# Two layers on one core: where layer 1's output weights are folded, and when its first queries are made

## The chip, the cores and the metric

The kernel runs on one core of a Trainium2 chip. The metric is the device time of one execution in microseconds, lower is better. Before the change three executions took 1293.99, 1299.66 and 1301.15 us; the median is 1299.66.

## What is computed

Two transformer layers, all in float32, over 2 sequences of 1024 tokens with 256 features. Each layer adds an attention and a feed-forward network, both fed with the same normalized input. Layer 1's attention compresses keys and values to 64 numbers for each token (`kv`) and has 16 heads:

```
xn = layernorm(x)
q  = rmsnorm(xn @ wq_a.T) @ wq_b.T            # 16 heads: 128 plain + 64 rotated
kv = rmsnorm((xn @ wkv_a.T)[..., :64])        # shared by all heads
q_abs  = einsum(q_nope, q_absorb)             # 64 per head
scores = (q_abs . kv + rope(q_pe) . rope(k_pe)) * SCALE      # causal
attn   = softmax(scores)
x = einsum('bhst,btc->bhsc', attn, kv)
x = einsum('bhsc,hdc->bhsd', x, out_absorb)   # 64 -> 128 per head
attention = x.reshape(b, s, 16 * 128) @ wo.T  # -> 256
ffn = bitlinear(sigmoid(bitlinear(xn, w1)) * bitlinear(xn, w2), w3)
```

The last two lines of the attention are both linear, with nothing between them. So `out_absorb` and `wo` can be multiplied into one matrix of 64 x 256 for each head. That product of weights is one of the things that the change moves.

## The kernel before

The program is written in an order fixed by hand: inside `manual_schedule` each engine runs its instructions in the order in which the code issues them. It has two scopes, with their own pools in SBUF and PSUM. The first holds layer 0, layer 1's feed-forward network and the preparation of layer 1's attention. The second holds layer 1's attention. A tile of the second scope may lie where tiles of the first lay, and then it waits for their last readers.

**The end of the first scope.** A list `fill` holds the items of layer 1's feed-forward network, first the products with w1 and w2 (`up`, L686), then those with w3 (`down`, L703). After each item, one piece from a second list, `side`, is issued (`pump`, then `side.pop(0)()`). In `side` stand, in this order: normalization and keys, the queries' transposes of batch 0 (`queries1`), the eight calls of `fold`, and at the end the last transposes and the first two queries.

**`fold(p)`** treats a pair of heads. It multiplies the query weights by `q_absorb` (L832, into `wm` and `w2`) and `out_absorb` by `wo` (L840, into `wvo`), and copies the three results from PSUM with `copy_out` (L95 on VectorE, L99 on ScalarE, in turn). `fold_load` fetches the factors of a pair over SP's queue (L822), two pairs ahead. The `wo` factors lie where layer 0's context lay.

**A query** (`Query`) belongs to 128 tokens and 8 heads. `project` makes it on TensorE (L143, L150) into a pair of PSUM banks; ScalarE copies it out (L169, L157, L172); `rotate` multiplies it by cosine and sine and adds (L173, L174, L178). Its parameter `engines` has GpSimd as default, for all three. The first two queries are made in the first scope by `query(0)` and `query(1)`, and use two `temp` tiles each as room. GpSimd runs nothing else there.

**The second scope.** 16 steps, one for each (batch, pair of token blocks i and 7 - i, 8 heads). A step has four cycles `c`; each cycle treats two heads for both blocks:

- `scores` (L1180): TensorE into a PSUM pair (tag `s`, two of them, also used by `project` and the outputs), then VectorE adds the mask and takes the maximum (L1187), then ScalarE's exp (L1191);
- `turn_over` (L1197): VectorE transposes the weights into `pT`, of which there are two, one for each of two successive steps;
- `values` (L1228): the product of the previous step's `pT` with `vrep`, into the PSUM tile `o` (four banks). The first step has no previous step, so it has no such product;
- `output` (L1255): the step before the previous one, multiplied by `wvo`.

`vrep` is filled with 32 copies of 64 KB on SP's queue (L1131) at the border of the scopes. It takes the place of `x_sb`, so it starts after the last store of x (L710).

Of the kernel before, what the change touches and what calls it, by code (L numbers as in the profile page):

```python
# [46 lines left out]
def two_layers(ctx: ExitStack, tc: tile.TileContext, a: dict, out: bass.AP):  # L47
# [42 lines left out]
    def copy_out(dst, src, scale=None):  # L90

        turn[0] += 1
        if turn[0] % 2:
            if scale is None:
                nc.vector.tensor_copy(dst, src)  # L95
            else:
                nc.vector.tensor_scalar(dst, src, scale, None, ALU.mult)
        else:
            nc.scalar.activation(dst, src, AF.Copy, scale=1.0 if scale is None else scale)  # L99
# [94 lines left out]
    with ExitStack() as scope:  # L194
# [10 lines left out]
        def ps_bank():  # L205
            return ps0.tile([P, SC], F32, tag="m", name="ps_m", bufs=3)
# [599 lines left out]
        def fold_load(p):  # L806
            if p == 0:


                wm = main.tile([P, 2, NPAIR, P], F32, tag="wA", name="wm")  # L810
                folded["wm"], folded["w2"] = wm[:, 0], wm[:, 1]
                nc.sync.dma_start(folded["w2"][:R2], a["wpe2"])
                folded["wvo"] = main.tile([P, NPAIR, E], F32, tag="wB", name="wvo")
                folded["wo"] = l0.tile([P, 4, 2, E], F32, tag="ctx_n", name="fold_wo")
            t0 = l0t.tile([P, S], F32, tag="head0", name="fold0", bufs=3)
            t, at = {}, 0
            for key, width in (("wbn", LQ), ("wka", LKV), ("wva", LKV)):
                t[key] = t0[:, at : at + 2 * width].rearrange("p (h r) -> p h r", h=2)
                at += 2 * width
            t["wo"] = folded["wo"][:, p % 4]  # L820
            for key in ("wbn", "wka", "wva", "wo"):
                nc.sync.dma_start(t[key], a[key][:, 2 * p : 2 * p + 2, :])  # L822
            folded[p] = t

        def fold(p):
            if p + 2 < NPAIR:
                fold_load(p + 2)
            t = folded[p]
            pm = ps_bank()
            for lo, n, at in ((0, P, 0), (P, R2, P)):  # L830
                for hh in range(2):
                    nc.tensor.matmul(  # L832
                        pm[P - n :, at + hh * LKV : at + (hh + 1) * LKV],
                        t["wbn"][:, hh, lo : lo + n], t["wka"][:, hh, :], start=True, stop=True,
                    )
            copy_out(folded["wm"][:, p, :], pm[:, :P])
            copy_out(folded["w2"][R2:, p, :], pm[R2:, P : 2 * P])
            pv = ps_bank()
            for hh in range(2):
                nc.tensor.matmul(  # L840
                    pv[hh * LKV : (hh + 1) * LKV, :E], t["wva"][:, hh, :], t["wo"][:, hh, :],
                    start=True, stop=True,
                )
            copy_out(folded["wvo"][:, p, :], pv[:, :E])


        with tc.manual_schedule():

# [243 lines left out]
            while fill:  # L1092
                k = len(fill)
                pump()
                for _ in range(-(-len(side) // k)):
                    side.pop(0)()
                if k == 17:
                    wpe = main.tile([P, 8 * E], F32, tag="wC", name="wpe")

                    maskw = wpe[:, NPAIR * P + 4 * P :]  # L1100
                    trig = wpe[:, NPAIR * P : NPAIR * P + 4 * P].rearrange("p (k t) -> p k t", k=4)
                    wpe = wpe[:, : NPAIR * P].rearrange("p (r c) -> p r c", r=NPAIR)
                    nc.sync.dma_start(wpe, a["wpe"])
                    for k_, i in enumerate((TB - 1, 0)):
                        for x_, key in enumerate(("cosq", "sinq")):
                            nc.sync.dma_start(
                                trig[:, 2 * k_ + x_], a[key][:, i * P : (i + 1) * P]
                            )

                    maskw = maskw.bitcast(BF16)  # L1110
                    nc.gpsimd.memset(maskw[:, : S - P], 0.0)
                    nc.gpsimd.tensor_copy(maskw[:, S - P :], maskz[:, SC - P :])

                    def query(k):
                        q = ready[steps[0]][k]
                        q.project(ps_pair())
                        q.rotate(
                            room=[temp("t").rearrange("p (r t) -> p r t", r=QP) for _ in range(2)]
                        )

                    ahead(0)
                    last = [lambda c=c, n=n: queries1(1, c, n) for n in (0, 4) for c in range(2)]
                    side += last[:2] + [lambda: query(0), last[2], lambda: query(1), last[3]]
            while side:
                side.pop(0)()

# [20 lines left out]
    with ExitStack() as scope:  # L1147
# [9 lines left out]

        class Step:
            pass

        def new_step(b, i, g):
            s = Step()
# [108 lines left out]
        with tc.manual_schedule():  # L1271
            prev, older = None, None

            def values(n0, n1):
                for sb in range(n0, n1):
                    product(prev, sb)

            for at in range(len(steps)):
                s = new_step(*steps[at])
                nxt = ahead(at + 1) if at + 1 < len(steps) else ()  # L1280
                for c in range(NCY):
                    wide = [2 * c, 2 * c + 1]
                    share = (c * NSB // NCY, (c + 1) * NSB // NCY) if prev is not None else (0, 0)
                    if c == 0 and older is not None:
                        normalize(older, 0)
                        fetch_x(older)
                    scores(s, 0, wide[:1])
                    if c == 0:
                        if older is not None:
                            normalize(older, 1)  # L1290
                        if prev is not None:
                            inverse(prev)
                        scores(s, 0, wide[1:])
                        scores(s, 1, wide)
                        values(*share)
                    else:
                        values(*share)
                        scores(s, 1, wide)
                        turn_over(s, 0, wide[0])
                        scores(s, 0, wide[1:])  # L1300
                    k = c // 2
                    q, after = None, []
                    if c % 2 == 0:
                        if nxt:
                            q = nxt[k]
                            q.project(pair("t"))
                    elif prev is not None:
                        t = pair("t")
                        if older is not None:
                            after.append(output(older, k, t[:, 0, :E]))  # L1310
                        after.append(inverse_T(prev, k, t[:, 1]))
                    if c == 0:
                        turn_over(s, 0, wide[0])
                        turn_over(s, 0, wide[1])
                        turn_over(s, 1, wide[0])
                        turn_over(s, 1, wide[1])
                    else:
                        turn_over(s, 1, wide[0])
                        turn_over(s, 1, wide[1])
                        for f in after:  # L1320
                            f()
                        turn_over(s, 0, wide[1])
                    if q is not None:
                        q.rotate()
                older, prev = prev, s

            for k in range(2):
                normalize(older, k)
                if k == 0:
                    fetch_x(older)  # L1330
            inverse(prev)
            mid = prev.nsb // 2
            values(0, mid)
            for k in range(2):
                t = pair("t")
                after = [output(older, k, t[:, 0, :E]), inverse_T(prev, k, t[:, 1])]
                for f in after:
                    f()
                if k == 0:
                    values(mid, prev.nsb)  # L1340
            normalize(prev, 0)
            mid = (prev.nsb + NSB) // 2
            values(prev.nsb, mid)
            t = pair("t")
            output(prev, 0, t[:, 0, :E])()
            values(mid, NSB)
            normalize(prev, 1)
            t = pair("t")
            output(prev, 1, t[:, 0, :E])()
# [67 lines left out]
```

## Time and profile before

| | us |
|---|---|
| median of three executions | 1299.66 |
| the profiled execution | 1296.76 |
| its span, first to last instruction | 1293.8 |
| TensorE busy | 1254.8 |
| VectorE busy | 743.9 |
| ScalarE busy | 640.9 |
| GpSimd busy | 486.6 |
| granted TensorE clock, mean | 0.996 |

The profile comes from one execution. The rows of the timeline read: start in us, duration in us, engine, line of the program, operation, what is written and read, shapes, count; in brackets the idle time of that engine ahead of the row and what ended it. A float32 matmul appears as two records. Shapes such as 128*64 are the rows and columns of TensorE's array that it uses. PE is TensorE, DVE VectorE, ACT ScalarE, POOL GpSimd, SP the engine that issues most transfers. A row that merges several records ("x8") gives the time from the first one's start to the last one's end, and records of TensorE overlap.

### The profile page before, as it was taken

What the parts mean: (1) busy time and instruction counts of PE and PEld (TensorE: products, weight loads), DVE (VectorE), ACT (ScalarE), POOL (GpSimd) and SP (SyncE); (2) the same over time, 40 slices, a digit from 0 to 9 for tenths busy, and PEclk for the clock granted to TensorE, in tenths of its full rate; (3) what the DMA queues carried; (4) which work ended last, traced back from release to release, by engine and by line L of the source; (5) the groups of instructions that cost most, each with busy time, mean ns of one, the idle gap of its engine ahead of it and who ended that gap; (6) DMA issues with size and microseconds to landing.
All of it is one profiled execution on the core that took longest, in us unless ns stands there. A gap on an engine that the chain in (4) does not pass through costs nothing. (4 is left out here: it accounts for less than half of the span.)

```text
span 1293.8 us, 36603 instructions
## 1 busy us (share of the span) xinstructions
PE 1254.8 (97%) x15774; PEld 790.3 (61%) x15774; DVE 743.9 (57%) x1873; ACT 640.9 (50%) x1228; POOL 486.6 (38%) x512
## 2 busy tenths in 40 slices
PE   8999999999999999999998899999999999999997
PEld 6554644545546445365585567677666677777665
DVE  5956545655456564134335666676566666766663
ACT  4465456375465444433323555555555555555541
POOL 6662325253233221103315543354345434544320
PEclk9999999999999999999999999999999999999999
DMA  6421301001001000002124100000001000000000
GB/s 187 127 56 51 90 1 26 14 13 17 9 1 26 26 1 21 17 1 80 48 86 76 20 19 7 26 11 15 21 8 27 7 28 10 27 11 7 23 7 23
DMA packets 66113, 41.10 MB, mean 32 GB/s; under 512 B 37857, under 2 KB 63329, under 8 KB 65825
## 3 DMA queue, kind: packets, MB, share of 16 engines
q1 hardware_dynamic: 64960, 36.69, 11.2%
q8 instruction: 123, 2.02, 0.7%
q10 hardware_dynamic: 704, 1.05, 0.2%
q0 software_dynamic: 288, 1.05, 0.2%
q14 instruction: 38, 0.30, 0.1%
HBM read 26.18 MB, written 10.49 MB: 28 GB/s over the span
## 5 line engine op out<-in xcount | busy, mean ns | idle before, releaser
L1191 ACT ACTIVATE p<-p,nmax 128x1024 f32<-128x1024 f32 (+7 forms) x256 | 197.2, 771 | 205.3 <-DVE nmax L1187 204.5
L1180 PE MATMUL ps_s<-kT,qc 128*128 128x512 f32 (+3 forms) x768 | 278.6, 497 | 14.2 <-DVE nmax L1187 13.0
L1187 DVE CUSTOM_DVE_ANT_0 p<-ps_s,wpe 128x1024 f32<-128x1024 f32 (+7 forms) x256 | 184.8, 744 | 182.6 <-PE ps_s L1180 177.3
L461 ACT ACTIVATE p<-ps_s 128x1024 f32<-128x1024 f32 (+1 forms) x192 | 153.3, 808 | 166.7 <-PE ps_s L454 161.8
L1180 PEld LDWEIGHTS ps_s<-kT,qc 128*128 128x128 f32 x768 | 130.9, 190 | 123.2 <-issue 90.7
L1197 DVE STREAM_TRANSPOSE pT<-p 128x1024 f32<-128x1024 f32 (+7 forms) x256 | 186.5, 758 | 13.2 <-ACT p L1191 13.2
L413 PE MATMUL ps_m<-head,head 16*128 16x512 f32 (+3 forms) x672 | 177.8, 533 | 1.0 <-DVE nmx L424 0.6
L454 PE MATMUL ps_s<-head,head 17*128 17x512 f32 (+3 forms) x768 | 164.5, 533 | 0.0
L1228 PE MATMUL ps_o<-pT,vrep 32*64 32x128 f32 x9216 | 151.2, 275 | 4.8 <-DVE rinv L1202 2.6
L178 POOL TENSOR_TENSOR qc<-t,t 32x512 f32<-32x512 f32 x120 | 152.1, 1268 | 8.1
L1228 PEld LDWEIGHTS ps_o<-pT,vrep 32*64 32x64 f32 x9216 | 134.8, 131 | 32.2 <-issue 23.8
L464 POOL TENSOR_SCALAR_AFFINE_SELECT p<-p 128x256 f32<-128x256 f32 x128 | 53.5, 422 | 224.7 <-ACT p L461 223.5
L173 POOL TENSOR_TENSOR t<-t,cosq 128x512 f32<-128x512 f32 x28 | 35.6, 1272 | 259.7 <-issue 144.2
L413 PEld LDWEIGHTS ps_m<-head,head 16*128 16x128 f32 x672 | 67.7, 183 | 84.7 <-issue 27.8
L686 PE MATMUL ps_m<-xnT,w 128*128 128x512 f32 x192 | 92.3, 608 | 0.0
L429 DVE TENSOR_REDUCE nmx<-ps_m 128x1 f32<-128x512 f32 x112 | 72.2, 685 | 32.6 <-PE ps_s L454 24.6
L424 DVE CUSTOM_DVE_ANT_0 junk<-ps_m,maskz,nmx 128x512 f32<-128x512 f32 (+3 forms) x112 | 57.6, 548 | 47.1 <-PE ps_s L454 29.8
L479 PE MATMUL ps_o<-p,v 128*32 128x512 f32 (+3 forms) x768 | 81.6, 498 | 0.0
L567 PEld LDWEIGHTS ps_m<-wpr,hT 128*128 128x128 f32 x512 | 59.9, 191 | 17.9 <-DVE nmx L429 6.8
L424 DVE CUSTOM_DVE_ANT_0 junk<-ps_m,maskz 128x512 f32<-128x512 f32 (+3 forms) x112 | 50.5, 487 | 29.3 <-PE ps_s L454 24.6
L567 PE MATMUL ps_m<-wpr,hT 128*128 128x128 f32 x512 | 66.6, 282 | 0.0
L1255 PE MATMUL ps_t<-wvo,xT 128*128 128x256 f32 x256 | 62.6, 387 | 3.5 <-DVE nmax L1187 2.6
(179 smaller groups left out, 1739.4 us busy)
## 6 DMA issues: line engine op xcount, KB each, us to landing
stage<-rows SPq DMA_DIRECT2D x96, 64.0 KB, 3.1
rows<-proj SPq DMA_DIRECT2D x23, 256.0 KB, 2.4
w<-in_w SPq DMA_DIRECT2D x3, 768.0 KB, 5.1
x_sb<-in_x SPq DMA_DIRECT2D x4, 512.0 KB, 5.3
x<-x_sb SPq DMA_DIRECT2D x4, 512.0 KB, 3.2
fold_wo<-in_wo SPq DMA_DIRECT2D x8, 256.0 KB, 3.4
vrep<-kv SPq DMA_DIRECT2D x32, 64.0 KB, 2.1
xin<-x SPq DMA_DIRECT2D x16, 128.0 KB, 2.2
```

The source lines that it names most:

```text
L178: (even, odd)[x].tensor_tensor(self.qc[64 + 32 * x : 96 + 32 * x, hh], t1[at : at + 32], t2[at : at + 32], ALU.add,)
L413: nc.tensor.matmul(t[:, :w], quad(q, c, D0)[:, i * P : (i + 1) * P], quad(k, c, D0)[:, k0 : k0 + w], start=True, stop=True, tile_position= ...
L424: nc.vector.tensor_tensor_reduce(junk[:, :w], t[:, :w], maskz[:, SC - w :], -1.0, dst if k0 else 3.0e38, ALU.add, ALU.min, dst,)
L454: nc.tensor.matmul(t[:, c % 2, :w], quad(k, c, D0 + 1)[:, j * P : (j + 1) * P], quad(q, c, D0 + 1)[:, at : at + w], start=True, stop=True, ...
L461: nc.scalar.activation(p[:, pair[0] : pair[0] + 2, :w], t[:, :, :w], AF.Exp)
L567: nc.tensor.matmul(po[:, :P], f["h", hc // 2][:, hc % 2, t * P : (t + 1) * P], wpr[:, hc, cols], start=(hc == 0), stop=(hc == NH0 - 1),)
L686: nc.tensor.matmul(pw, w1t[f"w{i + 1}"][:, kc, hc * P : (hc + 1) * P], xnT1[n // 2][:, kc, (n % 2) * SC : (n % 2 + 1) * SC], start=(kc == ...
L1180: nc.tensor.matmul(sc[:, j * SC + n0 : j * SC + n1], s.q[k].qc[:, h // QP, h % QP, :], kT[:, s.b * S + n0 : s.b * S + n1], start=True, sto ...
L1187: nc.vector.tensor_tensor_reduce(p, sc[:, j * SC : j * SC + w], maskw[:, S - w :], -1.0, 3.0e38, ALU.add, ALU.min, nmax,)
L1191: nc.scalar.activation(p, p, AF.Exp, bias=nmax, scale=-1.0, accum_out=s.rsum[:, k, h : h + 1])
L1197: nc.vector.transpose(s.pT[:, at, h, :], s.p[k, h])
L1228: nc.tensor.matmul(s.o[64 * hh : 64 * hh + 64, c, k * P : (k + 1) * P], vrep[32 * c : 32 * c + 32, s.b * 32 + sb, :], s.pT[32 * c : 32 * c ...
```

## The change

Three edits.

1. `fold` no longer makes `wvo`, and `fold_load` no longer fetches its two factors (`wva`, `wo`).
2. A new function `output_weights` fetches both factors over GpSimd's queue, in five transfers of 512 KB, into a tile of the tag `pT`, which has two buffers, ahead of the first step. It returns eight pieces, one for each pair of heads, which multiply them into the PSUM tile `o`, and `take`, with which ScalarE copies the result to `wvo`. In the first step `fill` issues a piece at three places of cycles 1 and 3 and at two places of cycle 2; `take` follows the step.
3. Among the last pieces of `side`, `query(0)` and `query(1)` each change places with the transposes that stood ahead of them.

```diff
@@ fold_load
-                folded["wvo"] = main.tile([P, NPAIR, E], F32, tag="wB", name="wvo")
-                folded["wo"] = l0.tile([P, 4, 2, E], F32, tag="ctx_n", name="fold_wo")
...
-            for key, width in (("wbn", LQ), ("wka", LKV), ("wva", LKV)):
+            for key, width in (("wbn", LQ), ("wka", LKV)):
...
-            t["wo"] = folded["wo"][:, p % 4]
-            for key in ("wbn", "wka", "wva", "wo"):
+            for key in ("wbn", "wka"):
@@ fold
-            pv = ps_bank()
-            for hh in range(2):
-                nc.tensor.matmul(
-                    pv[hh * LKV : (hh + 1) * LKV, :E], t["wva"][:, hh, :], t["wo"][:, hh, :],
-                    start=True, stop=True,
-                )
-            copy_out(folded["wvo"][:, p, :], pv[:, :E])
@@ the last pieces of side
-                    side += last[:2] + [lambda: query(0), last[2], lambda: query(1), last[3]]
+                    side += [last[0], lambda: query(0), last[1], lambda: query(1)] + last[2:]
@@ second scope
+        def output_weights():
+
+            t = att.tile([P, NSB, NH2, 32], F32, tag="pT", name="wov", bufs=2)
+            t = t.rearrange("p n h q -> p (n h q)")
+            wo = t[:, : NH * E].rearrange("p (h e) -> p h e", h=NH)
+            wva = t[:, NH * E : NH * (E + LKV)].rearrange("p (h d) -> p h d", h=NH)
+            nc.gpsimd.dma_start(wva, a["wva"])
+            for h in range(0, NH, 4):
+                nc.gpsimd.dma_start(wo[:, h : h + 4], a["wo"][:, h : h + 4])
+            folded["wvo"] = main.tile([P, NPAIR, E], F32, tag="wB", name="wvo")
+            pv = ps.tile([P, 4, SC], F32, tag="o", name="ps_wvo").rearrange(
+                "p k (x e) -> p (k x) e", e=E
+            )
+
+            def product(p):
+                for hh in range(2):
+                    nc.tensor.matmul(
+                        pv[hh * LKV : (hh + 1) * LKV, p, :], wva[:, 2 * p + hh, :],
+                        wo[:, 2 * p + hh, :], start=True, stop=True,
+                    )
+
+            def take():
+                for k in range(0, NPAIR, 4):
+                    nc.scalar.copy(folded["wvo"][:, k : k + 4, :], pv[:, k : k + 4, :])
+
+            return [lambda p=p: product(p) for p in range(NPAIR)], take
@@ the steps
+            fold, fold_take = output_weights()
+
+            def fill():
+                if c > 0 and fold:
+                    fold.pop(0)()
...
                         values(*share)
+                        fill()
                         scores(s, 1, wide)
+                        fill()
                         turn_over(s, 0, wide[0])
                         scores(s, 0, wide[1:])
+                        if c != 2:
+                            fill()
...
+                if at == 0:
+                    fold_take()
```

## The prediction

> **What bounds the kernel now.** I read the page first: busy shares, then the 40 slices.
>
> ```profile
> PE 1254.8 (97%) x15774; PEld 790.3 (61%) x15774; DVE 743.9 (57%) x1873; ACT 640.9 (50%) x1228; POOL 486.6 (38%) x512
> ...
> PE   8999999999999999999998899999999999999997
> ```
>
> TensorE is busy 97% of the span, and the only dips are the first slice, slices 22 and 23 (679 to 744 us) and the last. Work taken from TensorE counts nearly one for one, unless it lies in a dip; work put into a dip may be free. Both edits lie around slice 22, so I asked for the busy time of two stretches: the fold of the weights, and layer 1's first step up to its first product with the values.
>
> ```profile
> core 0: us, PE busy (x) PEld busy (x) DVE busy (x) ACT busy (x) POOL busy (x), PEclk, DMA share, GB/s
> 636.50:659.50 23.00, 23.00 (x158) 15.56 (x157) 6.97 (x18) 4.82 (x14) 10.48 (x16) 1.00 0.54 164
> 684.86:722.64 37.78, 29.68 (x124) 16.00 (x124) 24.70 (x53) 19.32 (x43) 19.03 (x17) 0.95 0.43 77
> ```
>
> The fold keeps TensorE busy 23.00 of 23.00 us. The first step leaves it idle 8.1 of 37.78 us: no earlier step exists whose value products could fill it. There the order of events is set by the loop maximum (DVE L1187), exp (ACT L1191), transpose (DVE L1197), with TensorE waiting for a PSUM pair. The timeline shows how that step starts:
>
> ```profile
> 683.69 5.20 POOL L178 TENSOR_TENSOR qc<-t 32x512 f32<-32x512 f32 x4
> ...
> 685.33 3.67 PE L1180 MATMUL ps_s<-kT,qc 128*128 128x512 f32 x8 [0.48 <-DVE x_sb L708]
> ...
> 688.93 1.22 DVE L1187 CUSTOM_DVE_ANT_0 p<-ps_s,wpe 128x1024 f32<-128x1024 f32 x1 [3.74 <-POOL qc L178]
> ...
> 690.08 1.22 DVE L1187 CUSTOM_DVE_ANT_0 p<-ps_s,wpe 128x1024 f32<-128x1024 f32 x1
> ...
> 691.36 1.16 PE L143 MATMUL ps_t<-qnT,wm 64*128 64x128 f32 x16 [0.43 <-DVE nmax L1187]
> ```
>
> The scores begin at 685.33, yet the first maximum begins at 688.93, 0.04 us after GpSimd ends the second query's rotation (683.69 + 5.20 = 688.89). GpSimd holds it up, and the next projection (L143) then waits for the second maximum.
>
> [...] the granted clock is 0.50 from about 706.4 to 709.7 and again from 723.6 to 726.7, after gaps of 2.9 and 1.8 us. [...] the two 512 KB loads on POOL's queue here took 6.1 us in the crowded start, 0.83 us of POOL each.
>
> **Part 1, the fold loses its output product.** The product of a pair of heads (L840) is two matmuls of 128x256, 4 records; all eight make 32. One fold, TensorE's records alone:
>
> ```profile
> 639.56 0.76 PE L832 MATMUL ps_m<-fold 128*128 128x64 f32 x5
> 640.06 0.43 PE L840 MATMUL ps_m<-fold_wo,fold 128*64 128x256 f32 x1
> 640.15 0.34 PE L832 MATMUL ps_m<-fold 128*64 128x64 f32 x3
> 640.32 0.60 PE L840 MATMUL ps_m<-fold_wo,fold 128*64 128x256 f32 x3
> 640.85 0.70 PE L686 MATMUL ps_m<-xnT,w 128*128 128x512 f32 x1
> ```
>
> The first half's product starts at 640.06 beside the remaining L832 records; the second half's starts at 640.32, [...] and the next work starts at 640.85. A 256-wide record costs 0.216 us (L1255: eight in 1.73 us), so the second half takes 0.43 us[...]. Without L840 that next work could start at 640.32 + 0.10. Gain 0.43 us a fold, times 8: **-3.5 us**. Bounds: the whole stretch 640.06 to 640.85, 0.79 x 8 = -6.3; and -2.5, if fold 7 has to wait up to 1 us for its load, which is issued behind the wpe loads (651.40 now, first use 657.0, landing 3.4). I keep -3.5. Removed as well: 8 evictions of about 0.40 us (DVE 0.42, ACT 0.38) and 16 loads on SP (0.43 each): nothing gained, as DVE and ACT are busy 7 and 5 of 23 us and SP only queues; if TensorE did not cover them they would be worth 1.6 us per engine.
>
> **Part 2, the queries one item sooner.** In TensorE's order each query passes one item, a queries1 transpose group and a w3 product: 667.05 minus 665.27 = 1.78 us. GpSimd's two rotations run back to back, 7.8 us each (673.22 to 688.89), so both end 1.78 sooner relative to the stage's end, at 687.1. It is no new engine: these rotations are on GpSimd now. Their ACT copies move with them into time when ACT is idle (7.4 us before 670.23). No DMA moves in the program; SP's sine and cosine loads, whose first starts at 688.92, are released sooner. The next wait is then TensorE: the first head's scores are there about 1.92 us after 685.33 (694.34 to 696.26 elsewhere), at 687.25, so the first maximum gains 1.7. The second needs the second head (685.33 + 8 x 0.43 + 0.2 = 689.0) and gains only 1.1; the projection waits for that one: **-1.15 us**. Ends: 0 if TensorE proves to be the later anyway, -1.7.
>
> **Part 3, what the first step receives.** Eight pairs, [...] an estimate of 0.6: 4.8 us of TensorE. The idle time that covers them: the third pair and after have 2.9 us (702.0 to 704.9); before L1180 at 696.24 and 697.54 there are short waits for ACT and DVE; at c = 3 they are 0.9 and 0.5 us. Following the chain, only the pair before scores at 714.57 comes out late, by 0.2 us, and the maximum of that head is not due until 717.01. So nothing; without cover, +4.8.
>
> Each product is a new wait: for POOL's loads. POOL reaches them after its rotation, about 687.1; five issues x 0.83 end near 691.3, and the next rotation on POOL is due at 697.6, so nobody behind them suffers. By then the DMA engines also carry the last x store (512 KB) and from 691 the copies to vrep (0.6 of the engines). At the 300 GB/s that the store shows, wva, the first wo chunk and the store (1.57 MB) take 5.2 us from 688.5, so [...] the first product can run at about 695.2. TensorE reaches it after that cycle's first scores, 694.34 - 1.15 + 1.7 = 694.9. It then waits 0.3 us; queued behind it are the scores of both blocks, for which DVE has some 0.8 us of slack. I take **+0.4**, ends 0 and +12. vrep now lands at 716.3 and is needed at 722.6: six us of cover. The two evictions of 1024 columns on ACT, about 1.0 us each (from 0.58 for 512), find it idle from 719.5 to 722.0: nothing, up to +1 if the exps slip behind them.
>
> [...] A halved window of 3.3 us costs about 1.65 us; the profile shows two on the path (L1180's four records at 704.90 take 2.60 instead of 1.73; the value products at 722.64 take 3.81 instead of 2.32). The gap before 704.9 shrinks to about 2.2 us; the one at 720.2 does not shrink[...]. I take **-0.9**, ends 0 and -3.1.
>
> Sum: -3.5 - 1.15 + 0.4 - 0.9 = **-5.15 us**. The profiled execution took 1296.76 (span 1293.8 and 2.96 around it), so 1291.6 for a run like it. That run lies 2.9 below the median shown; the four executions average 1297.9. A new median should follow that average, not the luckier run: 1297.9 - 5 = **1293**.
>
> **Rivals.** *Everything goes further*: the full 6.3 of the fold, 1.7 and both clock windows, -11.1: 1287. [...] against it: the records of the second half account for the stretch. *The work only moves*: 4.8 of TensorE uncovered, 1298. For it: the gaps are scattered; against it: 8.1 us idle. *A short wait for the factors* of 2 to 5 us: 1295 to 1298. *The wait takes the gain's place and more*: [...] If they get the 100 GB/s that vrep gets, wva and wo's first chunk take 10 us and each later chunk 5, TensorE stalls in program order at products 1, 3 and 5, and vrep itself passes its deadline: +12, net +7, so 1305. It decides from landings after about 695.8, one us for one us; by 701 the gain is gone. Against it: six tenths of the engines' time leave room. *It doesn't do what it says*: rotation already on GpSimd is no gain, and is counted as none.
>
> **Numbers.** This measurement can tell about 0.5% (6.5 us) from no change; the forecast is 0.51% below the median, on the edge. Forecast 0.62, of which 0.36 under 1293.2; further 0.11; only moves 0.09; short wait 0.09; long wait 0.09. Faster 0.36 + 0.11 = 0.47; same 0.26 + 0.18 = 0.44; slower 0.09. The range 1287 to 1299.5 holds all but the long wait and the tails.
>
> **What would show it.** Right: ffn item to ffn item in the fold falls from 3.11 to about 2.7 us; the first maximum follows the scores by 1.9 us with TensorE as releaser; eight pairs of 128x256 records in a first step no longer than 37.8 us; ACT's two evictions before 722. Wrong: TensorE idle ahead of the first product with a DMA as releaser, vrep landing after 722, or the fold's step unchanged.

## The result, and the profile after

Six executions of the changed kernel took 1286.76 to 1294.09 us, median 1288.53; six of the kernel before 1293.99 to 1301.15, median 1298.88. The ratio is 0.9934, with a 95% interval of 0.9908 to 0.996: faster by 0.66%. Seven further executions beside 55 of the kernel before gave 0.9935 (0.9911 to 0.9958). The forecast was 1293.0, the range 1287 to 1299.5: the direction held and the median lies in the range, but two of the sum's terms were the wrong size, one of them by more than three microseconds, and it is the width of the range that took this in.

The profiled execution took 1294.09 us (span 1292.4), the longest of the six. The page, its busy line and the row of TensorE's 40 slices:

```profile
PE 1257.9 (97%) x15774; PEld 792.0 (61%) x15774; DVE 742.6 (57%) x1869; ACT 641.5 (50%) x1226; POOL 489.2 (38%) x517
...
PE   8999999999999999999999999999999999999997
```

The dip in slices 22 and 23 is gone, with the same 15774 matmul records: work has moved into it, none has been removed. The busy times of the two stretches (the fold up to the next item; the first step up to its successor's first value product), columns as before:

```profile
640.15:659.70 19.55, 19.55 (x127) 14.65 (x126) 5.26 (x14) 3.37 (x10) 10.49 (x16) 1.00 0.37 109
685.04:720.98 35.94, 32.47 (x157) 16.69 (x157) 24.98 (x53) 21.36 (x45) 20.16 (x20) 1.00 0.68 154
```

The fold's stretch is shorter by 3.45 us and still full. The first step is 1.84 us shorter although TensorE has 33 more records in it (157 against 124); it is now idle 3.5 us there instead of 8.1, and the mean clock is 1.00 instead of 0.95.

One fold, TensorE alone:

```profile
642.77 0.93 PE L829 MATMUL ps_m<-fold 128*128 128x64 f32 x8
643.63 0.70 PE L686 MATMUL ps_m<-xnT,w 128*128 128x512 f32 x1
```

From the fold's first record to the next item's it takes 0.86 us, where it took 1.29: 0.43 less, eight times 3.4. The start of the first step:

```profile
685.51 4.19 PE L1197 MATMUL ps_s<-kT,qc 128*128 128x512 f32 x12 [0.47 <-DVE x_sb L708]
...
687.60 0.62 POOL L1157 DMA_DIRECT2D wov<-in_wva  x1 [0.30 <-POOL qc L178]
687.70 1.23 DVE L1204 CUSTOM_DVE_ANT_0 p<-ps_s,wpe 128x1024 f32<-128x1024 f32 x1 [2.33 <-PE ps_s L1197]
...
689.22 1.22 DVE L1204 CUSTOM_DVE_ANT_0 p<-ps_s,wpe 128x1024 f32<-128x1024 f32 x1 [0.29 <-PE ps_s L1197]
```

The releaser of the first maximum is no longer GpSimd's `qc` but TensorE's `ps_s`. It starts 2.19 us after the scores instead of 3.60; the second maximum 3.71 instead of 4.75. The second row shows GpSimd going from the rotation straight to the loads. Where those are needed:

```profile
693.49 1.88 PE L1197 MATMUL ps_s<-kT,qc 128*128 128x512 f32 x4
695.98 0.65 PE L1167 MATMUL ps_wvo<-wov 128*64 128x256 f32 x4 [0.61 <-DMA wov<-in_wo]
696.56 0.71 PE L1197 MATMUL ps_s<-kT,qc 128*128 128x128 f32 x4
697.20 0.65 PE L1167 MATMUL ps_wvo<-wov 128*64 128x256 f32 x4
```

The first product waits 0.61 us for `wo`'s first chunk, and the scores queued behind it come later by that and by the product's own 0.58 (695.98 to 696.56).

The span alone hides most of this. Before its fold begins (640.10 against 636.44) the changed kernel's profiled execution has already lost 3.7 us, in code that is the same. The reason is in the granted clock. A halved window is a stretch of 3.4 us in which the granted clock is 0.50. That execution has them at 74, 81, 477 and 1269 us, the profiled one of the kernel before at 75, 706 and 723; two more ahead of the fold, at half of 3.4 us each, make 3.4 of the 3.7. To leave them out, the table counts from the last w3 product to the projection after the second step's first value products (L143), the work between being the same but for the edits. The column "windows" is the time with a halved clock in that stretch.

| kernel | this stretch, us | windows in it, us |
|---|---|---|
| before, four profiles | 41.52, 44.35, 41.52, 41.55 | 6.6, 13.4, 6.6, 6.7 |
| changed, two profiles | 38.19, 38.03 | 0, 0 |

Queries only (below) has this stretch without a halved window, at 37.44 us in both of its profiles (in the first 722.65 - 685.21). With the 1.04 us of the sooner queries added, that makes 38.5 for the kernel before, so its two windows cost 3.0 of the 41.5.

### The profile page after: what moved, and what is told of

Same layout as the page of the kernel before. It is cut to its first block, busy times and chain, and to the rows that moved or that the text cites. A ratio compares the mean times of both kernels' runs of the same rounds, so it can differ in the third digit from the quotient of the medians.

```text
span 1292.4 us, 36588 instructions
## 1 busy us (share of the span) xinstructions
PE 1257.9 (97%) x15774; PEld 792.0 (61%) x15774; DVE 742.6 (57%) x1869; ACT 641.5 (50%) x1226; POOL 489.2 (38%) x517
## 4 chain that ended last, share of the span: by engine, by line
PE 87%; DVE 6%; issue 3%; ACT 2%; POOL 1%; DMA 1%; DVEq 0%; ACTq 0%; POOLq 0%
PE ps_s L1197 16%; PE ps_m L413 12%; PE ps_o L1245 11%; PE ps_m L686 7%; PE ps_o L479 6%; PE ps_m L567 5%; PE ps_t L150 4%; PE ps_m L536 4%; PE ps_t L1272 4%; PE ps_m L703 3%; PE ps_t L143 3%; PE ps_m L338 2%; DVE p L1204 2%; DVE pT L1214 1%; PE ps_m L726 1%
## 5 line engine op out<-in xcount | busy, mean ns | idle before, releaser
L178 POOL TENSOR_TENSOR qc<-t,t 32x512 f32<-32x512 f32 x120 | 152.2, 1268 | 8.1
```

The source lines that it names most:

```text
L178: (even, odd)[x].tensor_tensor(self.qc[64 + 32 * x : 96 + 32 * x, hh], t1[at : at + 32], t2[at : at + 32], ALU.add,)
```

## The experiments

The executions of one kernel differ by up to 14 us (88 of the kernel before), and the mean granted clock listed with each explains most of it. A straight line through 202 executions, with one slope for all kernels and a height for each, leaves 0.84 us of scatter: 1.08 us for each 0.001 of clock. The height is the time at full clock; what remains of a difference is clock. The kernel with late loads (below) is left out: 12 of the 17.1 us of halved clock in its profile fall into a wait, so the line does not hold for it. The raw executions at clock 1.000 agree: four of the kernel before took 1290.55 to 1291.85 us, four of the changed one 1286.76 to 1288.59.

| kernel | runs | mean us | mean clock | against before, us | of it at full clock |
|---|---|---|---|---|---|
| before | 88 | 1298.1 | 0.9935 | | |
| changed | 13 | 1290.1 | 0.9975 | -8.1 +- 1.4 | -3.8 +- 0.5 |
| fold only | 17 | 1292.3 | 0.9966 | -5.9 +- 1.3 | -2.6 +- 0.5 |
| queries only | 22 | 1295.3 | 0.9950 | -2.8 +- 1.0 | -1.3 +- 0.4 |
| before, eight idle products | 22 | 1297.1 | 0.9952 | -1.1 +- 1.5 | +0.8 +- 0.4 |
| products in one piece | 6 | 1291.8 | 0.9960 | -6.4 +- 1.3 | -3.7 +- 0.7 |
| products twice | 22 | 1294.6 | 0.9956 | -3.5 +- 1.3 | -1.3 +- 0.4 |
| later place, warm end | 12 | 1290.9 | 0.9959 | -7.2 +- 1.8 | -4.6 +- 0.5 |

The bounds are for 95%. They do not cover what differs from one set of executions to another: the changed kernel's two sets (six and seven) lie 1.1 us apart at full clock, so a difference of less than about 1 us in the last column is not shown by it alone.

**The changed kernel again.**

> The changed kernel itself, beside the others. Theory A (removed work plus closed gaps): 8 to 10 us under the kernel before, in two nearly equal parts: about 4.5 us of work (3.5 from the fold, 1 from the start of the first step), the rest because halved-clock windows near 706 and 723 us no longer occur. Rival B (the windows fall anywhere by chance and the gaps have nothing to do with it): over more runs the difference shrinks to 4.5 us, and windows near 700 to 725 us show up in this kernel too.

Median 1289.80 us (1288.40 to 1293.06), ratio 0.9935 (0.9911 to 0.9958). The difference is 7.7 us by the means of these executions, just short of the 8 to 10 expected, and did not shrink to 4.5; its profile has no halved window in the first step. Over all 13 executions theory A's split stands roughly: 3.8 us of work and 4.3 of clock.

**Each half alone.** Fold only is the changed kernel with

```diff
-                    side += [last[0], lambda: query(0), last[1], lambda: query(1)] + last[2:]
+                    side += last[:2] + [lambda: query(0), last[2], lambda: query(1), last[3]]
```

and queries only is the kernel before with the opposite edit.

> The fold's product moved to the first step, the two queries in their old places. Theory A: the 3.5 us of the fold and most of the clock stay, the start of the first step loses 1.0 us again: 7 to 8.5 us under the kernel before; first maximum again released by GpSimd, about 4.0 us after the last w3 product. Rival C (the sooner queries carry the gain): no more than 4 us under it.

> The kernel before with the two queries one item sooner, the fold as it was. Theory A: the first maximum comes 1.4 us sooner and the first step's second projection 1.0 us sooner, 1 us in all; the gap ahead of the scores near 704 us stays at 2.9 us and the clock is halved there as before: 0 to 2 us under the kernel before. Rival C: 4 us or more under it.

Fold only: median 1292.95, ratio 0.9951 (0.9934 to 0.9968), 5.9 us under the kernel before, less than theory A's 7. Its timeline of VectorE has GpSimd back as the releaser of the first maximum:

```profile
686.72 1.23 DVE L1204 CUSTOM_DVE_ANT_0 p<-ps_s,wpe 128x1024 f32<-128x1024 f32 x1 [3.77 <-POOL qc L178]
```

Queries only: median 1295.24, ratio 0.9977 (0.9963 to 0.9991). At full clock the halves give -2.6 and -1.3, together -3.9, and the whole change -3.8: they add up, so in this neither needs the other. The queries' part is 2.8 us in all, more than A's 0 to 2, because 1.5 us of it is clock; the halved window that A expected in this kernel did not come. Rival C (4 us or more for it) is out.

**The gaps filled, and nothing saved.** The kernel before, with matmuls of the same shape at the eight places:

```diff
+                        nc.tensor.matmul(
+                            warm_o[hh * LKV : (hh + 1) * LKV, p, :], ones[:, :LKV],
+                            kT[:, p * E : (p + 1) * E], start=True, stop=True,
...
                         values(*share)
+                        fill()
                         scores(s, 1, wide)
+                        fill()
...
+                        if c != 2:
+                            fill()
```

> The kernel before with eight pairs of matmuls of the same shape (64 columns, 256 wide, ones times keys, result read by nobody) at the eight places of the first step, and nothing else changed; it does more work than the kernel before. Theory A: the gaps shrink, the halved windows at 706 and 723 us go, and the kernel is 2 to 4 us faster for more work. Rival B: 0 to 1 us slower. Rival D (the pieces lengthen the step): 3 to 5 us slower.

Median 1296.84, ratio 0.9994 (0.9977 to 1.0011): neither faster nor slower. At full clock the pieces cost 0.8 us, so rival D is out; the clock gives back 1.8. That the whole would be 2 to 4 us faster did not come true. The gap ahead of the scores near 704 us is filled as meant:

```profile
705.13 1.98 PE L1180 MATMUL ps_s<-kT,qc 128*128 128x512 f32 x4 [0.70 <-DVE nmax L1187]
```

This kernel gives a term of my sum its size, though: fold only should be -3.5 + 0.8 = -2.7 at full clock, and is -2.6.

**The products in one piece** at the end of the first step, ahead of the copies to `wvo`:

```diff
-                if c > 0 and fold:
+                if False:
...
                 if at == 0:
+                    for f in fold:
+                        f()
                     fold_take()
```

> The changed kernel, but the eight products are issued together at the end of the first step, ahead of the copies to wvo, and none in the gaps. Theory A (the gaps hide the products and their filling keeps the clock up): TensorE gets 8 x 0.6 = 4.8 us in one piece, of which some 2 us fit into the wait ahead of the second step's scores; the gap near 703 us is 2.9 us again, so halved windows come back: 3 to 6 us slower than the changed kernel, 2 to 5 us under the kernel before. Rival B (it only matters that the fold lost them): as the changed kernel, within 1.5 us.

Median 1291.82, ratio 0.9951 (0.9932 to 0.9971); 1.7 us above the changed kernel by the means, the same at full clock. My expectation of 3 to 6 us failed, in both of its parts. TensorE's timeline:

```profile
703.81 1.98 PE L1197 MATMUL ps_s<-kT,qc 128*128 128x512 f32 x4 [2.90 <-DVE nmax L1204]
...
713.83 3.67 PE L1167 MATMUL ps_wvo<-wov 128*64 128x256 f32 x32
717.43 1.13 PE L1197 MATMUL ps_s<-kT,qc 128*128 128x512 f32 x2
```

Side by side the eight take 3.60 us (713.83 to 717.43), 0.45 each instead of 0.58 apart. They delay the second step's scores, of which VectorE waits for 1.35 us; the stretch of the table above takes 38.97 us, 0.9 more than the changed kernel's. So by one or two profiles of each, placing the pieces in the gaps is worth about 1 us, not 4.8; the executions at full clock, with bounds of some 0.8, don't tell it from nothing. And the gap of 2.90 us is open again, with a clock of 1.00 after it: the scores take 1.98 us.

**The loads late.** Theory and slow rival of the prediction in one: the five loads are issued behind the rotation of the next step's first query.

```diff
+            def load():
+                nc.gpsimd.dma_start(wva, a["wva"])
...
                     if q is not None:
                         q.rotate()
+                    if at == 0 and c == 0:
+                        fold_late()
```

> The changed kernel, but POOL issues the five loads behind the rotation of the second step's first query, some 17 us later (about 704.5 instead of 687.6). Theory: the first product waits for its factors, one us for one us: landing at about 711, TensorE idle from 696 to 711, so the first step is 13 to 16 us longer; the kernel is 12 to 18 us slower than the changed one and slower than the kernel before. Rival (the other engines go on and absorb it): less than 8 us slower than the changed one.

Median 1309.02, ratio 1.0082 (1.0058 to 1.0106); by the means 18.7 us above the changed kernel, just past the expected 18. TensorE:

```profile
694.23 1.88 PE L1200 MATMUL ps_s<-kT,qc 128*128 128x512 f32 x4
711.80 1.12 PE L1170 MATMUL ps_wvo<-wov 128*64 128x256 f32 x4 [15.69 <-DMA wov<-in_wo]
```

The wait is 15.7 us, 15.1 more than in the changed kernel, and the stretch of the table is 17.5 longer: one for one, and then the halved clock on top (this first product takes 1.12 us instead of 0.65). The clock is halved from 699.8 to 716.9, for 12 of these 17 us while TensorE waits in any case. So the mechanism of the slow rival exists at its price, and the loads' early place keeps it off.

**The products twice**, at the same places (`fold[0]()` ahead of `fold.pop(0)()`).

> The changed kernel with every one of the eight products issued twice at its place (the second overwrites the first with the same values), so 4.7 us more of TensorE. Theory A: the first gaps (0.4 us of TensorE waiting for VectorE at 697 us and later 0.7 at 704) cover at most half; the step is 1 to 3 us longer and the kernel 0 to 3 us slower than the changed one. If a product cost its full time the kernel would be 4.7 us slower; if all were free, 0.

Median 1294.88, ratio 0.9971 (0.9955 to 0.9986). By the means it is 4.5 us above the changed kernel, more than expected; at full clock 2.5. In its profile

```profile
699.84 1.08 PE L1167 MATMUL ps_wvo<-wov 128*64 128x256 f32 x8
700.85 1.98 PE L1197 MATMUL ps_s<-kT,qc 128*128 128x512 f32 x4
```

the pairs take 1.02 us instead of 0.58, 3.5 more in all, and the stretch of the table 40.20, 2.1 more. The gaps thus covered the products once, but a second time only to two fifths.

**A later place, and a warm end.** In cycle 1 the first product goes behind the scores of the small block; and six matmuls stand where the last value products wait for a reciprocal.

```diff
                         values(*share)
-                        fill()
+                        if c > 1:
+                            fill()
                         scores(s, 1, wide)
...
+                        if c == 1:
+                            fill()
...
+            t = pair("warm")
+            for k in range(6):
+                nc.tensor.matmul(t[:, k % 2, :E], ones, kT[:, :E], start=True, stop=True)
```

> The changed kernel with two edits. First, in cycle 1 the first product is issued behind the scores of the small block instead of ahead of them (and a fourth place follows), so its wait for the loads, 0.6 us, holds up nothing that VectorE needs: 0.3 to 0.8 us less in the first step. Second, six matmuls (ones times keys, read by nobody) stand in the last steps' wait for VectorE's reciprocal, 2.6 us ahead of the value products near 1268 us, where four of the six profiles have a halved window. Theory A: no window at 1268 us, 1 to 1.5 us less on average from that, 1.5 to 2 us under the changed kernel in all. Rival B (windows are not tied to gaps): a window at 1268 us as often as before and 0 to 0.8 us under the changed kernel.

Median 1290.37, ratio 0.9945 (0.9926 to 0.9963). Against the changed kernel the means say +0.9 with bounds that overlap by far: not shown to be better. At full clock it is the fastest of all, 0.9 us under the changed one, which is no more than two sets of one kernel differ by. The step does what was meant:

```profile
691.10 2.62 PE L1197 MATMUL ps_s<-kT,qc 128*128 128x512 f32 x8
693.65 0.65 PE L1167 MATMUL ps_wvo<-wov 128*64 128x256 f32 x4
694.31 1.98 PE L1197 MATMUL ps_s<-kT,qc 128*128 128x512 f32 x4
```

There is no wait for the loads, and the stretch takes 37.48 us, 0.6 less. Its one profile has no window near 1268 us, but neither have several profiles of kernels without the edit (all four of the kernel before, the changed kernel again, products in one piece), and its mean clock is not higher. Whether the warm end helps stays open.

**Where the clock falls.** Three more profiles of the kernel before and one more of queries only, with no edit.

> The kernel before, one more profile, to see where the clock is halved. Theory A (its first step draws the windows): one or two windows between 685 and 727 us, as in its first profile (706 and 723), on top of those near 52, 75, 82, 477 and 1268 us that all kernels share. Rival B (no tie to the first step): none there in two of the three looks, as in seven of the eight profiles of the kernels with an edit.

> As the look before it: theory A one or two halved windows between 685 and 727 us, rival B none in two of three looks.

> As the two looks before it: theory A one or two halved windows between 685 and 727 us, rival B none in two of three looks.

> The kernel before with the two queries one item sooner, one more profile. All four profiles of the kernel before have the clock halved after the 2.9 us gap ahead of the scores near 704 us; the first profile of this kernel has the same 2.9 us gap and no halving. Theory A1 (the sooner start of the step takes the halving away, whatever the later gap): none between 685 and 727 us again. Theory A2 (the 2.9 us gap draws it and the first profile was luck): a halved window near 706 us.

All three further profiles of the kernel before have two or three halved windows in the first step, as its first profile had; rows of 1 us from the second of them (columns: TensorE busy, granted clock, DMA share, GB/s):

```profile
709.00:710.00 1.00, 0.81 (x2) 1.00 0.55 86
710.00:711.00 1.00, 1.00 (x3) 0.72 0.84 131
711.00:712.00 1.00, 1.00 (x3) 0.50 0.46 71
```

The scores come back from their gap at 709.20 and run at half speed from 710.4. The same stretch of queries only in its second profile:

```profile
703.00:704.00 1.00, 0.00 (x0) 1.00 0.58 91
704.00:705.00 1.00, 0.00 (x0) 1.00 0.70 106
705.00:706.00 1.00, 0.91 (x2) 1.00 0.62 97
706.00:707.00 1.00, 1.00 (x3) 1.00 0.71 112
```

Two empty rows, the same gap of 2.90 us, and then full clock, as in its first profile. Rival B is out for the first step: windows there in four of four profiles of the kernel before, and in one of nine of the kernels with an edit whose loads are not late (fold only, at 690 us, in the early gaps that the sooner queries shorten). Not every execution of the kernel before has them, though: a single window of 3.413 us lowers the mean clock to 0.9987, and four of its 88 ran at 1.000. And the cause that I gave, a long gap draws a window, is not enough: queries only and products in one piece keep the gap of 2.90 us and have no window after it. By the expectation's terms A1 is upheld against A2; but its reason, the sooner start, is not shown by this, and the stretches below speak against it.

In each profile the halved windows start whole multiples of 3.413 us apart (kernel before: 74.67, 706.14 and 723.20 us, which is 185 and 5 such steps). So the span can be cut into stretches along this grid, which lies differently in each profile. For every stretch I took the share of the array in use: each matmul record with its rows times columns as a share of 128 x 128, for 0.216 us per 256 columns of its output (the eight records of 128x256 at L1255 near 772 us in the kernel before start 0.216 us apart). From 45 us on, the 14 profiles have 5013 such stretches at full clock, and 53 of them stand ahead of a halved one. A share of 0.36, a level fitted to these profiles, sorts all but eight: 46 of the 53 lie under it, and 4959 of the other 4960 above. From these shares the table counts, as an estimate of mine, at how many places of the grid out of 100 a stretch of the first step would lie under that level.

| profile | emptiest stretches as the grid lay | places out of 100 |
|---|---|---|
| before | 0.25 and 0.36, both followed by a halved one | 95 |
| queries only | 0.42 and 0.44 | 74 |
| products in one piece | 0.44 | 74 |
| fold only | 0.34, followed by a halved one | 26 |
| before, eight idle products | 0.57 | 24 |
| changed | 0.57 | 0 |

In the kernel before, one stretch takes in 2.2 us of the gap. In queries only the grid cuts the gap, at 702.92 (701.32 to 704.23) and in the second profile at 703.82 (702.19 to 705.09); in products in one piece it does so at 702.17 (700.91 to 703.81). So neither part lies under the level. By this estimate the place of the grid spared these kernels, and not the sooner queries: in this their profiles were lucky. In the changed kernel, with the late gaps filled and the early ones shortened, no place out of 100 puts a stretch under it. No run was made to test the level on other profiles.

## Why the prediction was right or wrong

- **Fold, -3.5:** from the fold's first record to the end of w3 the profiles give 48.42 and 44.94 us, -3.48. That the second half's two records of 0.216 us are the whole gain was read rightly (the 0.10 beside them is what the trace leaves of the 0.53 us from 640.32 to 640.85), and the bounds of -6.3 and -2.5 were not needed: fold 7 ran without a wait.
- **Queries, -1.15:** the first maximum gained 1.41 instead of 1.7, the second and the projection behind it 1.04; -1.3 +- 0.4 at full clock. TensorE was the next to be late, as said, though with 2.19 us from scores to maximum instead of 1.9.
- **The waits of the products, +0.4:** too small; the idle-product kernel gives 0.8, the profile 0.75 (37.44 us of the stretch in queries only, 38.19 in the changed kernel). The loads landed at 695.84 instead of 695.2 (this profile's last w3 product ends 0.2 later) and TensorE waited 0.61 instead of 0.3: one of the signs of being wrong, a DMA as releaser ahead of the first product, came in small. The 695.2 was itself not what its terms give: 688.5 + 5.2 is 693.7, which would have meant no wait; the 1.5 us above that were an estimate of mine that no trace shows. The step that failed is the 0.8 us of slack: the product itself (0.58 us) stands ahead of the same scores as its wait, and together they used it up.
- **Cover:** six microseconds for `vrep` were claimed. It landed at about 719.6 (the last issue at 717.5 plus 2.1), with the products due at 720.98: 1.4 us left, since the last x store, beside the loads, took 5.5 us instead of 3.2 and delayed its start. The two copies on ACT lay at 717.84 to 719.77, in its idle time.
- **Clock, -0.9:** this is the term that was mis-sized. It measured -4.3 (-8.1 less -3.8), beyond the end of -3.1 that I had given. I had counted two windows in one profile and let each vanish with a chance of some 0.3; they are in every profile of the kernel before, sometimes three, and in none of the changed kernel's. That explains about 3 us. The remaining 1.3 would lie in other windows, those ahead of the fold among them; with bounds of 1.4 us it may be nothing. That fuller gaps spare windows was my estimate, which the trace of the kernel before did not show; two readings behind the term were off as well. The gap ahead of the scores near 704 shrank to 0.70 us and not to 2.2 because five pairs come ahead of it. And the gaps of 2.9 and 1.8 us alone do not tell the cases apart, since queries only keeps the first of them at 2.90 us at full clock; what sorts them in these profiles is the share in use of a stretch of the grid (all but eight of 5013). (Of the four scores, 1.73 us is too short: at full clock they take 1.98.)
- **The base:** the mean of the four times shown, 1297.9, was a good base: 88 executions average 1298.1.

The forecast of 0.51% with a chance of 0.47 for "faster" was too careful for the same reason: work at full clock gave 0.3%, the clock the rest. Without the clock the sum was -4.25 us, and -3.8 was measured, so that part was right in its steps.

## What to carry to other kernels

Weigh a term by what repeats: take a clock that drops at one place of the program as part of that place's cost until further profiles say otherwise, and compare kernels at equal clock before explaining a few microseconds. In these traces a gap of 2.90 us stood ahead of a halved clock in four of four profiles of one kernel and in none of two of another; the changed kernel's first step, whose emptiest stretch along the grid had 0.57 of the array in use, had no halved window in two profiles. By the estimate above, it is the emptiest stretch of 3.413 us that is to be looked at, not the longest gap. Work moved from a saturated stretch into a latency-bound step was nearly free here once, up to the idle time counted there (0.8 us for eight products of 0.58); twice as much was not (2.1 us more in the step). The wait placed ahead of something urgent cost its own length and that of the instruction that waits (0.61 and 0.58 us); with it put behind, the stretch was 0.6 us shorter.

## What was not expected of the hardware

- TensorE's clock was halved near 75, 82 and 477 us, in most profiles, although its records left at most 0.2 us idle in the stretch ahead; near 52 us, in at least five of the 14, the idle time was 0.6 us. Many of these records are matmuls of 16 of the 128 rows, and the share of the array in use was 0.45 or less.
- In the first step of the kernel before, halving follows gaps of 1.2 to 2.9 us, for 3.4 us, once for 6.8; yet queries only and products in one piece have a gap of 2.90 us without it. In late loads it lasts 17.1 us, five steps of 3.413.
- Eight pairs of half-array matmuls take 0.45 us each side by side, and 0.58 between full-array work.
- Four loads of 512 KB issued together on GpSimd's queue landed after 9.0 us in the median (up to 11.5), beside a store and the `vrep` copies.
